# First loads in larger parts by two queues, second group's inputs turned early, all weight sums on GpSimd: a fused attention and feed-forward kernel

## The chip, the cores and the metric

The kernel runs on one core of a Trainium2 chip. The metric is the device time of one execution in microseconds (us). Five engines run their own instruction lists in order and meet only at semaphores: TensorE (PE; its weight loads are shown apart as PEld), VectorE (DVE), ScalarE (ACT), GpSimd (POOL) and SyncE (SP), which here issues nearly all transfers. Transfers are carried by 16 DMA engines that all issuing queues share.

## The reference

Sixteen sequences of 128 rows and 1024 columns pass a cross-attention block and a feed-forward block, each with a residual. All is float32.

```
x = x + Attention(layernorm(x), ctx, ctx)        # Wq, Wk, Wv, Wo with biases
x = x + scale * (x_ei(layernorm(x)) @ kernel)    # kernel is 0/1; inputs beyond 80% of x count -4 times

Attention: Q = query @ Wq + bq      (32 heads of 32)
           K, V = ctx @ Wk + bk, ctx @ Wv + bv   (8 heads, each for 4 query heads)
           softmax(Q K^T / sqrt(32)) V, then @ Wo + bo
```

## The kernel before

**Groups.** Two sequences make a group (`GB = 2`), so there are eight groups. For each group the kernel forms V and K from the context (`prep_v` L404, `prep_k` L393), Q from the normalized rows (`prep_q_plain` L419 for the first group, `prep_q` L485 after it), then softmax and the weighted sum for four pairs of sequence and half of the heads (`attend` L755), then the output projection (`out_proj` L623) and the feed-forward product (`ffn` L738). PE is kept busy by weaving: the projection and feed-forward products of one group are cut in pieces and laid between the softmax steps of another.

**What sets the order.** All instructions after the first loads are put out by hand. A `Stream` (L23) keeps a queue of generators and a list of events with due times. Each piece of PE work adds its estimated microseconds to `now`; an event is put out when `now` passes its due time. The due times thus decide only the place of an instruction in its engine's list. On the chip an engine goes through that list in order and waits wherever its semaphores are not there yet.

**Quadrants.** VectorE transposes blocks of 32 by 32. So that whole tiles can be turned this way, the context and the weights Wk and Wv are loaded by quadrants of 32 partitions: four transfers each (`load_ctx` L147, `load_by_quadrants` L155), every row in runs of 1 KB. `turn_ctx` (L344) turns half a sequence's context in one instruction; a pair of tiles `cT` holds a group's. Rows of x are normalized by `norm_x` (L387): two halves of statistics (L283), their sum (L287), an addition (L289), then `rs_a`, a power on GpSimd (L291), and the scaling on VectorE (L292). VectorE waits for GpSimd between L289 and L292. The first two groups turn x on PE (`turned` L330); later groups send it through DRAM and turn it on VectorE (`rows_x` L356, `through_dram` L302, `turn_x` L366).

**First loads (L185 to L201).** SP, ACT and GpSimd issue in turn: context of sequence 0, Wv in three cuts of its columns of chunks (`2, 4`), context of sequence 1, Wk in two cuts, then the rows of sequences 0 and 1 and the output bias by SP. The identity matrix is made on GpSimd after its share of the loads. Then SP loads eight pieces of Wq (512 KB each, `fetch` L220), four blocks of Wo (`load_o_part` L810), and the context of sequences 2 and 3.

**Weight sums.** Products of Q (from the second group on) and of the output projection use seven instead of eight block products (`seven` L462), with sums of weight blocks. `combine` (L776) forms four sums of a half of Wq or Wo, two instructions of 128x512 each, and stores them in DRAM by SP. Wo's first half (`sums_of_wo` L856), Wq's second half and Wo's second half are formed on GpSimd, Wq's first half on VectorE (`sums_of_wq` L895, L904). They run beside the first group's attention, as do the transposes of the second group's context (due times in L923, L926, L927) and the norms of its rows (L928).

**Third group.** During the second group's attention the rows of the third are loaded, normalized at due times of 10 and 14 us (`get_x` L875), sent through DRAM and turned at 30 to 36 us (`turn_rows` L882); its context is turned at 3.7 to 18 us (L939).

Of the kernel before, what the change touches and what calls it, by code (L numbers as in the profile page):

```python
# [17 lines left out]
P = 128  # L18
# [58 lines left out]
def once(fn, *args):  # L77
    fn(*args)
    yield 0.0
# [3 lines left out]
def kernel(  # L83
# [40 lines left out]
    ps_tp = ctx.enter_context(tc.tile_pool(name="ps_tp", bufs=2, space=PSUM))  # L124
    ps_sc = ctx.enter_context(tc.tile_pool(name="ps_sc", bufs=4, space=PSUM))

# [17 lines left out]
    def load_ctx(b, queues=(nc.sync,)):  # L147
        c_t = work.tile([P, NB, NC, 32], FP, tag="ctx", name=f"ctx{b}", bufs=2)
        src = key_value[b].rearrange("(t r) (k c f) -> k r t (c f)", r=32, k=NB, c=NC)
        for k in range(NB):  # L150
            dst = c_t[k * 32 : (k + 1) * 32].rearrange("r t c f -> r t (c f)")
            queues[k % len(queues)].dma_start(out=dst, in_=src[k])
        cs[b] = c_t

    def load_by_quadrants(dst, w, queues, *cuts):  # L155

        src = w.rearrange("(k c f) n -> k f c n", k=NB, f=32)
        n = 0
        for lo, hi in zip((0,) + cuts, cuts + (NC,)):
            for k in range(NB):  # L160
                queues[n % len(queues)].dma_start(
                    out=dst[k * 32 : (k + 1) * 32, lo:hi], in_=src[k][:, lo:hi]
                )
                n += 1

    def load_x(b, tag="row"):

        x_t = work.tile([P, D], FP, tag=tag, name=f"xn{b}", bufs=2)
        nc.sync.dma_start(out=x_t, in_=x[b])
        xns[b] = x_t  # L170
# [10 lines left out]
            )  # L181

    three = (nc.sync, nc.scalar, nc.gpsimd)  # L185
    load_ctx(0, three)
    load_by_quadrants(wv_sb, Wv, (nc.scalar, nc.gpsimd, nc.sync), 2, 4)
    load_ctx(1, three)
    load_by_quadrants(wk_sb, Wk, (nc.scalar, nc.gpsimd, nc.sync), 4)
    load_x(0)  # L190
    load_x(1)
    ident = const.tile([P, P], FP, name="ident")
    make_identity(nc, ident)
    minus_half = const.tile([P, 1], FP, name="minus_half")
    nc.gpsimd.memset(minus_half, -0.5)

    nc.gpsimd.dma_start(out=bkT, in_=bk)
    nc.gpsimd.dma_start(out=bv_b, in_=bv.partition_broadcast(P))
    nc.gpsimd.dma_start(out=bqT, in_=bq.rearrange("p (a g) -> p a g", a=NA))
# [573 lines left out]
            stream.later(0.7 + 2.4 * i, first)  # L773
        return pts

    def combine(w, k, part, engine=nc.gpsimd):  # L776

        if w == "q":

            a11, a12, a21, a22 = [part[r, o] for o in range(2) for r in range(2)]  # L780
            ops = [(a22, a21, a22, ADD), (a21, a11, a21, SUB), (a11, a22, a11, SUB), (a12, a12, a11, SUB)]
            order = (a22, a11, a21, a12)
        else:
            b11, b12, b21, b22 = [part[r, o] for r in range(2) for o in range(2)]
            ops = [(b11, b12, b11, SUB), (b12, b22, b12, SUB), (b22, b22, b11, SUB), (b21, b21, b22, SUB)]
            order = (b11, b22, b12, b21)
        for dst, left, right, op in ops:
            for h in range(2):
                cols = slice(h * HALF, (h + 1) * HALF)
                engine.tensor_tensor(dst[:, cols], left[:, cols], right[:, cols], op)  # L790
            yield
        for n, t in enumerate(order):
            nc.sync.dma_start(out=sums[w, n + 1, k], in_=t)
# [30 lines left out]
    with tc.manual_schedule():  # L824
# [8 lines left out]
        for grp in range(NGRP):  # L833
            os[grp] = out_proj(grp)
            if grp + 2 < NGRP:
                qs[grp + 2] = prep_q(grp + 2)
        for _ in range(RING):
            fetch()
        o_parts = [load_o_part(0)]

        def plain(a):
            return prep_q_plain(a, {(r, k): at_q[r, a, k] for r in range(2) for k in range(2)})
# [3 lines left out]
                turn_ctx(j, h)  # L846
            stream.add(prep_v(0, [j]))
        stream.add(prep_k(0))
        for j in range(GB):
            load_ctx(GB + j)  # L850
        stream.run(0.0, lambda: len(stream.queue) > 1)
        nc.vector.tensor_scalar_mul(bqs, bqT, scale)
        for j in range(GB):
            norm_x(j)

        def sums_of_wo():  # L856
            def inputs():
                for j in range(GB):
                    load_x(GB + j, "turn")
                load_ffn()  # L860

            def then():
                o_parts.append(load_o_part(1))

            stream.later(10.0, inputs)
            stream.later(8.0, lambda: spread(combine("o", 0, o_parts[0]), 3.3, then))

        stream.add(prep_x(0, 0), prep_x(0, 1), once(sums_of_wo), plain(0))
        stream.run(0.0, lambda: stream.queue)

        def norms(grp, *us):
# [3 lines left out]
        def get_x(grp):  # L875

            for j in range(GB if grp < NGRP else 0):
                b = grp * GB + j
                load_x(b, "turn")
                stream.later((10.0 if grp == 2 else 5.0) + 4.0 * j, lambda b=b: rows_x(b))  # L880

        def turn_rows(grp):  # L882
            for n, at in enumerate((30.0, 32.0, 34.0, 36.0)):
                stream.later(at, lambda n=n: turn_x(grp * GB + n // 2, n % 2))

        def get_ctx(grp):
# [8 lines left out]
        def sums_of_wq(k):  # L895
            def then():
                for _ in range(4):
                    fetch()
                if k == 1:
                    spread(combine("o", 1, o_parts[1]), 3.3)  # L900

            part = {(r, o): pieces[at_q[r, o, k]] for r, o in BLOCKS}
            if k == 0:
                spread(combine("q", k, part, nc.vector), 1.5, then)  # L904
            else:
                spread(combine("q", k, part), 3.3, then)

        def between(gen, n, fn, *args):

# [5 lines left out]
        for grp in range(NGRP):  # L915
            b0, b1, nxt = grp * GB, grp * GB + 1, grp + 1
            p0, p1 = b0 - 2, b0 - 1
            first, more = grp == 0, nxt < NGRP
            last = grp == NGRP - 1
            length = 17.4 if first else 23.2 if grp < NGRP - 2 else 21.0  # L920
            if first:
                stream.add(
                    once(prep_ctx, nxt, 12.5, 13.5),  # L923
                    between(plain(1), 9, sums_of_wq, 0),
                    once(sums_of_wq, 1),
                    once(turn_ctx, nxt * GB, 1),  # L926
                    once(turn_ctx, nxt * GB + 1, 1),  # L927
                    once(norms, nxt, 5.0, 10.0),  # L928
                    prep_k(nxt),
                    once(get_ctx, nxt + 1),  # L930
                    prep_v(nxt),
                    prep_x(nxt, 0),
                    prep_x(nxt, 1),
                    once(convert_ffn),
                    between(qs[nxt], 40, residuals, grp),
                )
            elif more:
                stream.add(
                    *([once(get_x, nxt), once(prep_ctx, nxt, 3.7, 8.0, 13.0, 18.0)] if grp == 1 else []),  # L939
                    once(turn_rows, nxt),  # L940
                    os[grp - 1],
                    once(get_ctx, nxt + 1),
                    prep_k(nxt),
                    once(load_residual, b0, 4.0),
                    prep_v(nxt),
                    qs[nxt],
                    once(get_x, nxt + 1),
                    once(prep_ctx, nxt + 1, 2.5, 7.0, 11.0, 16.0),
                    ffn(p0),
                    once(load_residual, b1, 2.0),  # L950
                )
                if nxt < NGRP - 1:
                    stream.add(ffn(p1))
            else:
                stream.add(
                    os[grp - 1],
                    mixed(ffn(p1 - 2), ffn_transpose(p0), 10, 2),
                    once(load_residual, b0, 2.0),
                    mixed(ffn(p0), ffn_transpose(p1), 8, 2),
                    once(load_residual, b1, 2.0),  # L960
                )
            if not more:
                for q in range(2 * NA):
                    b, a = grp * GB + q % GB, q // GB
                    start = stream.now
                    pts = attend(b, a, 15.0)
                    stream.later(15.0, lambda b=b, a=a, pts=pts: weighted(b, a, pts) or 1.0)
                    stream.run(start + 12.0)
                stream.drain()
                break  # L970
            for q in range(2 * NA):
                b, a = grp * GB + q % GB, q // GB
                start = stream.now
                pts = attend(b, a, length)
                if q == 2 * NA - 1:
                    stream.run(start + length - 2.0, lambda: stream.queue)
                else:
                    stream.run(start + length - 2.0)
                stream.run(stream.now, lambda: None in pts)
                weighted(b, a, pts)  # L980
                stream.now += 1.0
# [56 lines left out]
```

## Time and profile before

| | |
|---|---|
| median of 3 runs | 792.11 us (790.93 to 792.24) |
| the profiled execution's own time | 790.87 us |
| its span, first to last instruction | 789.1 us |
| PE busy | 767.6 us (97%) |
| DVE, ACT, POOL busy | 485.6, 322.7, 113.3 us |
| DMA, mean over the span | 241 GB/s |
| granted PE clock | full in every slice |

The profile page gives the busy time of each engine, the span in 40 slices, the chain of work that ended last, and groups of instructions by line. Its rows can be listed in order of time (the timeline): start, length, engine, line, operation, what is written and read, how many, and in brackets how long the engine sat idle before and what released it. A line with `SPq` or `DMA` is an issue or a transfer. All times count from the span's start.

### The profile page before, as it was taken

The page shows a single profiled execution, that of the slowest core. Times are in us where ns is not written, and L with a number is a line of the kernel's source. Part 1 is how long each engine was busy: PE and PEld are TensorE (multiplying, and loading weights), DVE is VectorE, ACT ScalarE, POOL GpSimd, SP SyncE. Part 2 cuts the span into 40 slices and gives each one's busy share as a digit, 9 for nine tenths or more (in the row PEclk, how much of TensorE's full clock was granted, in tenths as well). Part 3 has the DMA queues.
Part 4 walks back from the last instruction along what each step waited for, and adds up shares of the span by engine and source line. Part 5 has one row for each costly group of instructions (what it writes and reads, how often), then busy time and mean ns, then how long its engine had stood idle before and what let it go on. Part 6 is the DMA issues. An engine that isn't in the chain of part 4 may idle for free.

```text
span 789.1 us, 13748 instructions
## 1 busy us (share of the span) xinstructions
PE 767.6 (97%) x5024; PEld 572.0 (72%) x5024; DVE 485.6 (62%) x882; ACT 322.7 (41%) x1261; POOL 113.3 (14%) x142
## 2 busy tenths in 40 slices
PE   5998999999999999999999999999999999999997
PEld 4886884589746996479855898568974799546566
DVE  1258748756766667466684667755676756667442
ACT  0254754434344343344433444343434445466100
POOL 4143703020010102020020200102001200100300
PEclk9999999999999999999999999999999999999999
DMA  9999799987698776888788796977769567562512
GB/s 236 350 314 309 277 338 388 283 225 266 224 316 217 248 238 229 298 213 260 221 256 274 197 285 218 306 222 214 257 226 315 194 203 249 178 200 81 198 42 81
DMA packets 97828, 190.32 MB, mean 241 GB/s; under 512 B 8080, under 2 KB 56272, under 8 KB 97760
## 3 DMA queue, kind: packets, MB, share of 16 engines
q1 hardware_dynamic: 96128, 187.33, 74.2%
q0 software_dynamic: 528, 1.12, 0.6%
q10 hardware_dynamic: 1104, 0.98, 0.6%
q8 instruction: 40, 0.66, 0.3%
q14 instruction: 28, 0.23, 0.1%
HBM read 160.04 MB, written 29.36 MB: 240 GB/s over the span
## 4 chain that ended last, share of the span: by engine, by line
PE 84%; DMA 7%; DVE 3%; SPq 2%; POOL 1%; issue 1%; ACT 1%; POOLq 0%
PE f L323 15%; PE o_u L662 13%; PE q_u L451 12%; PE o_v L662 7%; PE tpp L601 6%; PE q_v L451 6%; PE v L323 5%; PE k L323 5%; PE sc L568 4%; PE av L611 4%; PE o_c L662 3%; PE q_c L451 3%; DMA wo<-in_L_xattn_Wo_dram 2%; SPq L225 1%; DMA piece<-in_L_xattn_Wq_dram 1%
## 5 line engine op out<-in xcount | busy, mean ns | idle before, releaser
L584 ACT ACTIVATE p<-sc,negm 128x128 f32<-128x128 f32 x512 | 181.5, 369 | 140.3 <-DVE negm L580 76.8
L603 ACT COPY pt<-tpp 128x512 f32<-128x512 f32 x128 | 74.5, 591 | 142.9 <-PE tpp L601 142.6
L580 DVE TENSOR_REDUCE negm<-sc 128x4 f32<-128x512 f32 x128 | 86.6, 679 | 53.7 <-PE sc L568 53.6
L584 ACT ACTIVATION_READ_ACCUMULATOR p<-sc,negm 128x1 f32 x512 | 105.4, 206 | 0.0
L323 PE MATMUL f<-wf_sb,x2l 128*128 128x512 f32 x256 | 104.8, 409 | 0.0
L323 PE MATMUL f<-wf_sb,x2h 128*128 128x512 f32 x256 | 100.5, 393 | 0.0
L596 DVE TENSOR_TENSOR p<-p,inv 128x512 f32<-128x512 f32 x128 | 91.9, 718 | 4.4
L451 PE MATMUL q_u<-t,piece 128*128 128x128 f32 x672 | 80.9, 275 | 0.0
L601 PEld LDWEIGHTS tpp<-ident,p 128*128 128x128 f32 x512 | 61.9, 141 | 25.6 <-issue 17.0
L601 PE MATMUL tpp<-ident,p 128*128 128x128 f32 x512 | 75.9, 273 | 4.5 <-DVE p L596 3.1
L451 PEld LDWEIGHTS q_u<-t,piece 128*128 128x128 f32 x672 | 77.9, 192 | 0.0
L180 POOL TENSOR_TENSOR x<-x,bo_b 128x256 f32<-128x256 f32 x64 | 55.1, 887 | 151.3 <-DMA x<-in_x_dram 99.4
L323 PE MATMUL v<-wv_sb,cT 128*128 128x256 f32 x256 | 61.4, 388 | 9.5 <-DMA wv_sb<-in_L_xattn_Wv_dram 7.4
L662 PE MATMUL o_v<-piece,s 128*128 128x512 f32 x128 | 60.4, 598 | 0.5 <-DVE x L676 0.5
L662 PE MATMUL o_u<-piece,s 128*128 128x512 f32 x128 | 59.1, 594 | 0.7 <-DVE x L676 0.7
L323 PEld LDWEIGHTS v<-wv_sb,cT 128*128 128x128 f32 x256 | 47.8, 194 | 16.3 <-DVE cT L349 9.4
L323 PE MATMUL k<-cT,wk_sb 128*128 128x256 f32 x256 | 58.1, 380 | 1.3 <-DVE cT L349 1.3
L662 PE MATMUL o_u<-piece,yT 128*128 128x512 f32 x128 | 58.5, 599 | 0.0
L323 PEld LDWEIGHTS f<-wf_sb,x2l 128*128 128x128 f32 x256 | 48.2, 188 | 10.4 <-issue 1.1
L323 PEld LDWEIGHTS k<-cT,wk_sb 128*128 128x128 f32 x256 | 47.9, 190 | 10.5 <-issue 2.6
L323 PEld LDWEIGHTS f<-wf_sb,x2h 128*128 128x128 f32 x256 | 48.2, 188 | 9.4 <-issue 0.5
L568 PEld LDWEIGHTS sc<-kT,qT 32*128 32x128 f32 x1024 | 31.4, 186 | 25.7 <-issue 25.7
(86 smaller groups left out, 936.3 us busy)
## 6 DMA issues: line engine op xcount, KB each, us to landing
piece<-o SPq DMA_DIRECT2D x64, 512.0 KB, 4.8
piece<-q SPq DMA_DIRECT2D x56, 512.0 KB, 5.1
piece<-in_L_xattn_Wq_dram SPq DMA_DIRECT2D x50, 512.0 KB, 5.3
piece<-in_L_xattn_Wo_dram SPq DMA_DIRECT2D x48, 512.0 KB, 4.6
xn<-in_x_dram SPq DMA_DIRECT2D x16, 512.0 KB, 6.8
x<-in_x_dram SPq DMA_DIRECT2D x16, 512.0 KB, 4.8
ctx<-in_ctx_dram SPq DMA_DIRECT2D x60, 128.0 KB, 7.0
out_dram<-x SPq DMA_DIRECT2D x15, 512.0 KB, 2.7
```

The lines of the kernel that those rows point to most:

```text
L180: lambda cut=cut: nc.gpsimd.tensor_add(x_t[:, cut], x_t[:, cut], bo_b[:, cut]) and None,
L225: nc.sync.dma_start(out=t.rearrange("p (c n) -> p c n", c=src.shape[1]), in_=src)
L323: nc.tensor.matmul(mm, lhsT=lhsT, rhs=rhs, start=k == 0, stop=k == n - 1)
L451: nc.tensor.matmul(mm if part is None else mm[:, part], lhsT=lhsT, rhs=rhs, start=start and n == k == 0, stop=k == len(some) - 1, skip_gro ...
L568: nc.tensor.matmul(tiles[i][:, g], lhsT=qT[rows, g], rhs=kT[rows, a, cols], start=True, stop=True,)
L580: nc.vector.tensor_reduce(negm, tile_, AX.X, ALU.max, negate=True)
L584: nc.scalar.activation(p[:, g], tile_[:, g], AF.Exp, bias=negm[:, g : g + 1], accum_out=total[:, g : g + 1],)
L596: nc.vector.tensor_mul(p, p, inv.unsqueeze(2).to_broadcast([P, NG, S]))
L601: nc.tensor.transpose(tp[:, g], p[:, g], ident)
L603: nc.scalar.copy(pt, tp)
L611: nc.tensor.matmul(mm[i * HD : (i + 1) * HD], lhsT=vs[b][:, h * HD : (h + 1) * HD], rhs=pts[i], start=True, stop=True,)
L662: nc.tensor.matmul(mm, lhsT=lhsT[:, 2 * k + c], rhs=w[:, c], start=start and k == c == 0, stop=k == c == 1, skip_group_check=True,)
```

## The change

Six edits, all of which act on what is put out before the third group's attention:

1. The first loads are issued by SP and ACT alone. Wv and Wk go in four parts of 256 KB each, without cuts. The rows of sequence 0 are issued before Wk, those of sequence 1 after it. The identity is made first of all on GpSimd.
2. The context of sequences 2 and 3 is loaded after six of the eight Wq pieces, before the last two and before Wo; the rows of sequences 2 and 3 directly after Wo.
3. The four transposes of the second group's context are put out while the first group's Q is formed (`prep_ctx, 1` beside `plain(0)`).
4. All sums of `combine` are formed on GpSimd, Wq's first half too.
5. The norms of the second group's rows come at other due times (12 and 24 us after the first attention step begins; before, 5 and 10 us after the second half of the first group's Q).
6. For the third group, rows are normalized 8 us later, context is turned at 5 to 24 us instead of 3.7 to 18, rows are turned 5 us later.

```diff
-    def load_by_quadrants(dst, w, queues, *cuts):
+    def load_by_quadrants(dst, w, queues):
...
-    three = (nc.sync, nc.scalar, nc.gpsimd)
-    load_ctx(0, three)
-    load_by_quadrants(wv_sb, Wv, (nc.scalar, nc.gpsimd, nc.sync), 2, 4)
-    load_ctx(1, three)
-    load_by_quadrants(wk_sb, Wk, (nc.scalar, nc.gpsimd, nc.sync), 4)
+    two = (nc.sync, nc.scalar)
+    load_ctx(0, two)
+    load_by_quadrants(wv_sb, Wv, two)
+    load_ctx(1, two)
     load_x(0)
+    load_by_quadrants(wk_sb, Wk, two)
     load_x(1)
...
-        for _ in range(RING):
+        for _ in range(RING - 2):
+            fetch()
+        for j in range(GB):
+            load_ctx(GB + j)
+        for _ in range(2):
             fetch()
         o_parts = [load_o_part(0)]
+        for j in range(GB):
+            load_x(GB + j, "turn")
...
-            stream.later(8.0, lambda: spread(combine("o", 0, o_parts[0]), 3.3, then))
+            stream.later(9.0, lambda: spread(combine("o", 0, o_parts[0]), 3.3, then))
-        stream.add(prep_x(0, 0), prep_x(0, 1), once(sums_of_wo), plain(0))
+        stream.add(prep_x(0, 0), prep_x(0, 1), once(sums_of_wo),
+            once(prep_ctx, 1, 5.0, 7.0, 9.0, 11.0), plain(0))
...
-                stream.later((10.0 if grp == 2 else 5.0) + 4.0 * j, lambda b=b: rows_x(b))
+                stream.later((18.0 if grp == 2 else 5.0) + 4.0 * j, lambda b=b: rows_x(b))
...
             for n, at in enumerate((30.0, 32.0, 34.0, 36.0)):
+                at += 5.0 if grp == 2 else 0.0
...
-            if k == 0:
-                spread(combine("q", k, part, nc.vector), 1.5, then)
-            else:
-                spread(combine("q", k, part), 3.3, then)
+            spread(combine("q", k, part), 2.7, then)
...
-                    once(prep_ctx, nxt, 12.5, 13.5),
+                    once(norms, nxt, 12.0, 24.0),
                     between(plain(1), 9, sums_of_wq, 0),
                     once(sums_of_wq, 1),
-                    once(turn_ctx, nxt * GB, 1),
-                    once(turn_ctx, nxt * GB + 1, 1),
-                    once(norms, nxt, 5.0, 10.0),
                     prep_k(nxt),
...
-    *([once(get_x, nxt), once(prep_ctx, nxt, 3.7, 8.0, 13.0, 18.0)] if grp == 1 else []),
+    *([once(get_x, nxt), once(prep_ctx, nxt, 5.0, 9.0, 14.0, 24.0)] if grp == 1 else []),
```

More of the change, by code (lines that the diff above doesn't have):

```diff
@@ L125 @@
     ps_sc = ctx.enter_context(tc.tile_pool(name="ps_sc", bufs=4, space=PSUM))
+    ident = const.tile([P, P], FP, name="ident")
+    make_identity(nc, ident)
+    minus_half = const.tile([P, 1], FP, name="minus_half")
+    nc.gpsimd.memset(minus_half, -0.5)
     wk_sb = const.tile([P, NC, KV], FP, name="wk_sb")
@@ L153, in load_ctx @@
         cs[b] = c_t
-    def load_by_quadrants(dst, w, queues, *cuts):
+    def load_by_quadrants(dst, w, queues):
         src = w.rearrange("(k c f) n -> k f c n", k=NB, f=32)
[L158 to L164, printed above, removed]
+        for k in range(NB):
+            queues[k % len(queues)].dma_start(out=dst[k * 32 : (k + 1) * 32], in_=src[k])
     def load_x(b, tag="row"):
@@ L181, in load_residual @@
             )
-    three = (nc.sync, nc.scalar, nc.gpsimd)
-    load_ctx(0, three)
-    load_by_quadrants(wv_sb, Wv, (nc.scalar, nc.gpsimd, nc.sync), 2, 4)
-    load_ctx(1, three)
-    load_by_quadrants(wk_sb, Wk, (nc.scalar, nc.gpsimd, nc.sync), 4)
+    two = (nc.sync, nc.scalar)
+    load_ctx(0, two)
+    load_by_quadrants(wv_sb, Wv, two)
+    load_ctx(1, two)
     load_x(0)
+    load_by_quadrants(wk_sb, Wk, two)
     load_x(1)
[L192 to L195, printed above, removed]
     nc.gpsimd.dma_start(out=bkT, in_=bk)
@@ L774, in attend, with combine @@
         return pts
-    def combine(w, k, part, engine=nc.gpsimd):
+    def combine(w, k, part):
         if w == "q":
@@ L789, in combine @@
                 cols = slice(h * HALF, (h + 1) * HALF)
-                engine.tensor_tensor(dst[:, cols], left[:, cols], right[:, cols], op)
+                nc.gpsimd.tensor_tensor(dst[:, cols], left[:, cols], right[:, cols], op)
             yield
@@ L848 @@
         stream.add(prep_k(0))
-        for j in range(GB):
-            load_ctx(GB + j)
         stream.run(0.0, lambda: len(stream.queue) > 1)
-        nc.vector.tensor_scalar_mul(bqs, bqT, scale)
         for j in range(GB):
             norm_x(j)
+        nc.vector.tensor_scalar_mul(bqs, bqT, scale)
         def sums_of_wo():
[L857 to L860, printed above, removed]
             def then():
                 o_parts.append(load_o_part(1))
-            stream.later(10.0, inputs)
-            stream.later(8.0, lambda: spread(combine("o", 0, o_parts[0]), 3.3, then))
-        stream.add(prep_x(0, 0), prep_x(0, 1), once(sums_of_wo), plain(0))
+            stream.later(10.0, load_ffn)
+            stream.later(9.0, lambda: spread(combine("o", 0, o_parts[0]), 3.3, then))
+        stream.add(
+            prep_x(0, 0),
+            prep_x(0, 1),
+            once(sums_of_wo),
+            once(prep_ctx, 1, 5.0, 7.0, 9.0, 11.0),
+            plain(0),
+        )
         stream.run(0.0, lambda: stream.queue)
```

## The prediction

> **What bounds the kernel now.** I read PE's waits first, then PE's timeline, then the stretches of the start.
>
> PE's waits over the whole span (total, times, longest; two more rows are of 0.5 and 0.3 us):
>
> ```profile
> PE v L323 <- DMA wv_sb<-in_L_xattn_Wv_dram: 7.4, 2, 7.0
> PE tpp L601 <- DVE p L596: 3.1, 2, 2.6
> PE v L323 <- DVE cT L349: 2.1, 1, 2.1
> PE tpp L601 <- DVE x2l L717: 1.4, 1, 1.4
> PE k L323 <- DVE cT L349: 1.3, 1, 1.3
> PE o_u L662 <- DVE x L676: 0.7, 1, 0.7
> PE o_v L662 <- DVE x L676: 0.5, 1, 0.5
> ```
>
> PE is the bound (767.6 of 789.1 us busy). Only these waits can be won, and the change reaches all but the 1.4 us, which lie at the end. PE's own list has the same instructions in the same order after the change, so its work costs the same. The waits' places, in PE's timeline:
>
> ```profile
> 6.99 3.61 PE L323 MATMUL v<-wv_sb,cT 128*128 128x256 f32 x8 [6.99 <-DMA wv_sb<-in_L_xattn_Wv_dram]
> ...
> 15.10 3.72 PE L323 MATMUL v<-wv_sb,cT 128*128 128x256 f32 x16 [2.07 <-DVE cT L349]
> 18.65 7.07 PE L323 MATMUL k<-cT,wk_sb 128*128 128x256 f32 x32
> ...
> 64.05 5.45 PE L323 MATMUL k<-cT,wk_sb 128*128 128x256 f32 x24 [1.29 <-DVE cT L349]
> ...
> 80.15 0.63 PE L601 MATMUL tpp<-ident,p 128*128 128x128 f32 x4 [2.65 <-DVE p L596]
> ```
>
> K of the first group begins at 18.65 with no wait; from there PE never idles 0.3 us until 64. So the whole start counts by one number: when K begins. After that: 1.29 and 0.45 + 2.65 us at 62 to 80, and 1.24 us at 136 to 142.
>
> **The start (edit 1).** Stretches: length, busy times, then granted clock, DMA share, GB/s:
>
> ```profile
> 2.00:10.00 8.00, 3.01 (x7) 2.50 (x8) 1.31 (x2) 0.00 (x0) 7.05 (x16) 1.00 1.05 246
> 10.00:16.00 6.00, 3.47 (x14) 2.28 (x14) 1.64 (x3) 1.28 (x1) 0.00 (x0) 1.00 1.11 216
> 38.00:42.00 4.00, 4.00 (x26) 3.28 (x28) 0.00 (x0) 0.79 (x3) 1.96 (x3) 1.00 1.08 199
> 21.00:31.00 10.00, 9.76 (x53) 8.47 (x53) 3.19 (x6) 3.06 (x6) 1.12 (x2) 1.00 1.10 348
> ```
>
> The DMA engines are full in all four, yet the rate differs: 246 GB/s with quadrant loads from three queues, 216 mostly from two, 199 from SP alone (context), 348 for Wq pieces on all 128 partitions in the same 1 KB runs. So the destination of 32 partitions sets the rate. [...] I take 208, between the one- and the two-queue row; bounds 199 and 239 (the mean from 2 to 17 us before).
>
> Data flows from 2.0 us. Wv has landed after 0.52 (context) + 1.05 + 0.13 MB (the bias, beside them): 2.0 + 1.70/0.208 + 0.25 (landing) = 10.4. V takes as long as K, whose 32 matmuls run from 18.65 to 25.56: 6.9 and, since the second context lands at 12.9 and is turned by 13.7, runs through: PE is ready for K at 17.4. Wk comes after the second context and the rows of sequence 0: 3.28 MB by quadrants, 0.52 MB of rows at 0.4 (the 406 GB/s of the rows before): 2.0 + 15.75 + 1.3 + 0.25 = 19.3. K begins at 19.3 instead of 18.65: **+0.65**. With 239 it is 17.3 (-1.35), with 199 it is 20.0 (+1.35). What is late next is Wk, because rows went in front of it: that alone costs 1.3. [...] The norms of both rows (statistics to scaling 3.3 us each, from 17.6 on) end near 24, before K does at 26.2: hidden; x1 lands by 20.6.
>
> **Order of pieces, early transposes (edits 2, 3).** Six Wq pieces, then 1 MB of context at 199 (5.3 us), lands near 36.5. Four transposes at 0.69 = 2.8 us fall into VectorE's empty stretch from 25.7 to 42.9 (17.3 us before the first maximum): free. The K wait of **1.29** goes. Wq's last two pieces come at 39, needed at 50; Wo's last part at 44.5 to 45.5 instead of 41.7, which delays GpSimd, not PE; the rows of sequences 2 and 3 behind it by 48 (1.3 us each), asked for at 56.6.
>
> **Sums on GpSimd (edits 4, 5).** The rows: VectorE's eight sum instructions cost 6.2 us there (mean 817 ns). GpSimd's timeline:
>
> ```profile
> 41.80 7.39 POOL L790 TENSOR_TENSOR wo<-wo,wo 128x512 f32<-128x512 f32 x6 [2.04 <-DMA wo<-in_L_xattn_Wo_dram]
> 57.52 2.65 POOL L790 TENSOR_TENSOR piece<-piece,piece 128x512 f32<-128x512 f32 x2 [8.33 <-PE q L323]
> ...
> 76.51 5.85 POOL L790 TENSOR_TENSOR piece<-piece,piece 128x512 f32<-128x512 f32 x4
> ```
>
> 1.23 us per instruction beside a quiet VectorE, 1.46 beside a busy one (single ones 1.27 or 1.72). [...]
>
> The danger is order. Each `rs_a` stands in GpSimd's list, and VectorE stands still until it is done. New list on GpSimd: 8 for Wo, 2 for Wq, `rs_a` of sequence 2, 10 for Wq, `rs_a` of sequence 3, 4 for Wq. On VectorE the norm of sequence 2 now stands after the fourth product with 1/sum (56.6 before), that of sequence 3 after the second one of the next step.
> - Wo's sums: 45.5 + 6 x 1.23 = 52.9, two more to 55.5. VectorE asks for the first `rs_a` at 58.3, so nobody waits: a cover of 2.8 us. Then GpSimd goes on at 58.9 with ten sums: 12.3 us and three meetings of 0.45 = 13.6, to 72.5.
> - VectorE meanwhile: scaling to 60.7, maxima from 61.0 (63.93 before), exponentials on ScalarE from 61.7, two products done by 67.3, statistics to 69.0. Then it stands until `rs_a` is done at 73.1, about 4 us. Behind it: scaling (to 74.8), fourth maximum (75.4), third product (76.7 with a meeting). Also ScalarE's fourth exponential stands behind that maximum.
> - PE: K from 60.77 for 6.9, then transposes and V between; it reaches the third transpose at 73.0 and waits to 76.7 (3.7 us). Fourth at 78.9, no more wait; the weighted sum at 80.3, where it was 81.57. So 1.29 + 0.45 + 2.65 of waits go, 3.7 come with small gaps between: **-1.25**. Bounds: ten sums at 1.23 give -2.6, at 1.6 (nearest the 1.72) +1.0.
>
> The weight sums themselves are ready earlier than before (last Wq sum 78.5 instead of 82.3), also Wo's second half (90 instead of 94.3). Meetings after 90 fall away: the 0.32 wait at 101 may go, **-0.2**. SP's queue: the stores of Wq's first sums hold it from 59 to 67.5; behind them stand four Wq pieces, needed at 84 and landing at 76, then context needed at 125.
>
> **Third group (edit 6).** PE at 136.7 waited 0.71 and at 141.8 waited 0.53, both for an addition that stood behind a norm (3.0 us from statistics to scaling) on VectorE. In the new list both additions stand ahead of the norms: **-1.2** (bounds -1.24 and 0). The price: rows of sequence 5 come back from DRAM behind eight context loads on SP, near 164; VectorE may stand 2 us from 162 for them, ahead of what PE needs at 168 (the next sums of rows at 176). Counted at nothing, up to 1 if they come at 167. Not seen in the trace.
>
> **Sum.** +0.65 - 1.25 - 0.2 - 1.2 = **-2.0 us**. The profiled span would go from 789.1 to 787.1, its own time from 790.87 to 788.9. The median of the runs is 792.11, so 790.1.
>
> **Rivals.**
> - *Two queues carry as much as three* (239 GB/s): K begins at 17.3, 2.0 better than forecast: 788.1. For it: 246 GB/s began as 237 in its first 2 us, when GpSimd's queue had hardly come in. Against it: 216 and 199.
> - *The gain becomes a new wait*: GpSimd's ten sums take 15 us instead of 13.6 (1.5 each, as in Wo's second half now), and the start runs at 199: 790.1 + 1.4 + 0.7 = 792.2, no difference that can be told. For it: the standing VectorE is the longest new wait and passes to PE one for one. Against it: while VectorE stands it meets nobody.
> - *Slower: the first loads.* [...] Each part of K's delay passes to PE. At 160 GB/s Wk lands at 2.0 + 20.5 + 1.55 = 24.0, +4.75 over the forecast: 794.9. It decides from 169 GB/s down (K at 22.9, total +1.6). For it: in the SP-only stretch single microseconds went to 173, and at 10 to 16 the rate fell as Wv and Wk came in. Against it: no stretch of 4 us lies under 199.
>
> **How the numbers follow.** A measurement of this kernel can tell 0.2% (1.6 us) from no change. Forecast 0.48 (of it 0.32 beyond 0.2%, 0.16 within), two queues as good as three 0.2 (faster), gain becomes a wait 0.12 (within), slow loads 0.2 (slower, with a late return of sequence 5 in the same share). So faster 0.52, same 0.28, slower 0.2. Low end: start at 239 (-2.0) and the sums at their best bound (-1.35) give 790.1 - 3.35, near 787.0; 5 in 100 lie below. High end: into the slow-loads case, 794.0, some 14 in 100 above.
>
> **What would show it.** K's first matmul: 19.3, released by Wk, not by context. No wait for cT at 62. VectorE idle some 4 us before the scaling of sequence 3, released by `rs_a`; the third transpose of that step waits about 3.7. No wait at L662 near 136 to 142. I am wrong if K starts past 22 or before 18, if VectorE stands at the first `rs_a` already (Wo later than 48), or if PE waits anew after 150.

## The result

The changed kernel takes 796.42 us (median of 4 runs, 795.53 to 797.32), the kernel before it, on the same chip, 791.56 us (790.93 to 792.24). The ratio is 1.0062, its 95% interval 1.0048 to 1.0076: slower by some 4.9 us, where 2.0 us faster was forecast. The profiled execution took 797.32 us with a span of 795.6 us.

### The profile page after: what moved, and what is told of

It reads as the page before. It is cut to its first block, busy times and chain, and to the rows that moved or that the text cites. A ratio compares the mean times of both kernels' runs of the same rounds, so it can differ in the third digit from the quotient of the medians.

```text
span 795.6 us, 13726 instructions
## 1 busy us (share of the span) xinstructions
PE 770.2 (97%) x5024; PEld 574.1 (72%) x5024; DVE 479.1 (60%) x874; ACT 322.4 (41%) x1261; POOL 119.1 (15%) x141
## 4 chain that ended last, share of the span: by engine, by line
PE 88%; DMA 5%; DVE 3%; POOL 2%; ACT 2%; issue 1%; ACTq 0%; SPq 0%; POOLq 0%
PE f L316 15%; PE o_u L655 14%; PE q_u L444 11%; PE o_v L655 7%; PE tpp L594 6%; PE q_v L444 6%; PE v L316 6%; PE k L316 5%; PE sc L561 4%; PE av L604 4%; PE o_c L655 3%; PE q L316 3%; PE q_c L444 2%; POOL piece L783 2%; DMA wv_sb<-in_L_xattn_Wv_dram 1%; DMA turn_x<-dram_x 1%
## 5 line engine op out<-in xcount | busy, mean ns | idle before, releaser
L316 PE MATMUL f<-wf_sb,x2l 128*128 128x512 f32 x256 | 105.4, 412 | 0.0
L316 PE MATMUL f<-wf_sb,x2h 128*128 128x512 f32 x256 | 101.1, 395 | 0.0
L594 PEld LDWEIGHTS tpp<-ident,p 128*128 128x128 f32 x512 | 62.5, 142 | 25.6 <-issue 17.1
L594 PE MATMUL tpp<-ident,p 128*128 128x128 f32 x512 | 76.3, 274 | 4.7 <-DVE p L589 3.3
L316 PE MATMUL v<-wv_sb,cT 128*128 128x256 f32 x256 | 62.4, 395 | 13.0 <-DMA wv_sb<-in_L_xattn_Wv_dram 13.0
L316 PEld LDWEIGHTS v<-wv_sb,cT 128*128 128x128 f32 x256 | 49.1, 199 | 19.3 <-issue 13.0
L316 PE MATMUL k<-cT,wk_sb 128*128 128x256 f32 x256 | 57.9, 380 | 0.8 <-DVE v L405 0.8
L316 PEld LDWEIGHTS f<-wf_sb,x2l 128*128 128x128 f32 x256 | 48.2, 188 | 11.0 <-issue 1.1
L316 PEld LDWEIGHTS f<-wf_sb,x2h 128*128 128x128 f32 x256 | 48.2, 188 | 10.2 <-issue 0.5
L316 PEld LDWEIGHTS k<-cT,wk_sb 128*128 128x128 f32 x256 | 47.9, 190 | 10.0 <-issue 2.6
```

Of the source, the lines that this page charges most:

```text
L316: nc.tensor.matmul(mm, lhsT=lhsT, rhs=rhs, start=k == 0, stop=k == n - 1)
L594: nc.tensor.transpose(tp[:, g], p[:, g], ident)
```

## The profile after

Line numbers are seven lower than before (L323 is now L316, L601 is L594). PE's waits over the whole span of the changed kernel:

```profile
PE v L316 <- DMA wv_sb<-in_L_xattn_Wv_dram: 13.0, 1, 13.0
PE tpp L594 <- DVE p L589: 3.3, 1, 3.3
PE q_c L444 <- DVE v L405: 1.8, 1, 1.8
PE tpp L594 <- DVE x2l L710: 1.4, 1, 1.4
PE k L316 <- DVE v L405: 0.8, 1, 0.8
PE av L604 <- ACT pt L596: 0.6, 1, 0.6
```

The forecast waits are gone: the K wait on `cT`, both waits at the additions, and 0.45 of the two transposes. One long wait of 3.3 us stands in for the 2.65, as forecast (3.7). Two rows are new: 13.0 us at the start for Wv, and 1.8 us before Q of the third group. The same places in PE's timeline (start, length, then what, and in brackets the wait ahead of it):

```profile
13.01 9.04 PE L316 MATMUL v<-wv_sb,cT 128*128 128x256 f32 x32 [13.01 <-DMA wv_sb<-in_L_xattn_Wv_dram]
22.86 7.14 PE L316 MATMUL k<-cT,wk_sb 128*128 128x256 f32 x32 [0.81 <-DVE v L405]
...
64.98 7.17 PE L316 MATMUL k<-cT,wk_sb 128*128 128x256 f32 x32
...
75.45 1.89 PE L316 MATMUL v<-wv_sb,cT 128*128 128x256 f32 x8
...
80.65 0.63 PE L594 MATMUL tpp<-ident,p 128*128 128x128 f32 x4 [3.30 <-DVE p L589]
81.11 3.03 PE L316 MATMUL v<-wv_sb,cT 128*128 128x256 f32 x8
...
177.29 2.94 PE L444 MATMUL q_c<-xT,piece 128*128 128x128 f32 x24 [1.78 <-DVE v L405]
```

Two things are to be seen besides the waits. K begins at 22.86, not at 19.3. And the same eight V matmuls take 1.89 us at 75.45 and 3.03 us at 81.11, just behind the long wait. Likewise V of the first group takes 9.04 us where 6.9 was reckoned: its first eight matmuls are 0.427 us apart, later ones 0.216. (The wait ahead of K names `v`, but that addition was over at 22.51; the last part of Wk landed at 22.77.)

PE's list is the same in both kernels, so each matmul can be set against its twin. How much later each place is reached, in the two profiled executions:

| place | shift after it | step's own part | forecast |
|---|---|---|---|
| K of the first group begins | +4.21 | +4.21 | +0.65 |
| second attention step done (85 us) | +4.35 | +0.14, of it half clock some +1.7 | -1.25 |
| weighted sum at 105 | +4.61 | +0.26 | -0.2 |
| additions at 140 and 145 | +2.84 | -1.77 | -1.2 |
| Q of the third group | +5.24 | +2.4 | 0, up to +1 |
| last matmul | +6.74 | +1.5, in the feed-forward products | 0 |

(Half clock is a stretch in which PE is granted half its clock; here 0.50 from 81.71 to 85.12. From the third transpose to the end of the step PE takes 4.53 us here, from 80.65 to 85.18, and 2.85 in e2, described below, which has no half clock there.)

The last row is not scatter between two executions. From 180 us on only the feed-forward products (`f`) go slower. Their rows on the two pages, first before, then after (busy us, mean ns of one):

```profile
L323 PE MATMUL f<-wf_sb,x2l 128*128 128x512 f32 x256 | 104.8, 409 | 0.0
L323 PE MATMUL f<-wf_sb,x2h 128*128 128x512 f32 x256 | 100.5, 393 | 0.0
...
L316 PE MATMUL f<-wf_sb,x2l 128*128 128x512 f32 x256 | 105.4, 412 | 0.0
L316 PE MATMUL f<-wf_sb,x2h 128*128 128x512 f32 x256 | 101.1, 395 | 0.0
```

From one start to the next it is 229.7 ns before and 233.4 after, the mean of 426 neighbouring pairs; the other products keep their pace (K 215.9 ns, V 216.8). The experiments below tell with which edit this goes.

The profile before was below all four timed runs of its kernel, and this one is the highest of its four: the profiles differ by 6.45 us, the medians by 4.9.

## Experiments

Each set shared one chip and the runs of the kernel before: 791.44 us (40 runs) for the first four kernels, 791.87 us (51 runs) for the next four, 791.98 us (20 runs) for the last four.

### The loads alone, and everything but the loads

`e1_loads_alone`: the kernel before with edit 1 only.

> The kernel before with edit 1 alone (two queues, 256 KB parts, rows ahead of Wk). Theory: the start is where the time went, because the last DMA ring to finish a part lags the mean by some 3 us and PE then starts with its clock at half: K of the first group starts at 22.9 as in the changed kernel, and the later waits stay as before (1.3 and 2.7 us near 64 and 80), so the time is that of before + 4.2 (795.8). Rival (the later edits are to blame, the start is absorbed by slack behind it): within 1.5 us of before.

Measured: 795.71 us (794.02 to 797.46), ratio 1.0062 (1.0046 to 1.0077). `e2_loads_undone`: the changed kernel with the first loads of before.

> The changed kernel with the first loads of before. Theory: V starts at 7.0, K at 18.7, so 4.2 us go: near 792.2, within 1 us of the kernel before, since the other edits lose as much as they win. Rival (the gains forecast for the other edits are there): 788 to 789.

Measured: 790.92 us (788.04 to 793.14), ratio 0.9994 (0.9983 to 1.0005). So edit 1 by itself costs what the whole change costs, and the other five edits together are worth 0.5 us by the medians, which this cannot tell from nothing. In e1's trace K begins at 20.72 and not at 22.9, so the start costs 2.1 us there; 0.45 of it is won back by 145 us, and 1.5 come after 180 us. The expected total was met with a part of it in another place. In e2's trace the shift against before is -0.97 us after the second attention step and -3.15 after the additions; Q of the third group gives 2.0 of it back (a wait of 1.4 and smaller ones), and after 180 us nothing is lost. The loads and the third group were thus separate losses.

**The slower feed-forward products come with edit 1.** From start to start they take 233.3 to 233.4 ns in the changed kernel, e1, e3 to e8 and e11, and 229.7 in before, e2, e10 and e12; that is 1.5 us in all. Of what edit 1 changes, e5 has three queues again, e6 the small parts and e7 the rows behind Wk, and all three are slow. What the slow kernels share, and the others lack, is the identity made ahead of the loads. In the code `ident` and `minus_half` (one column) are then also taken from the pool `const` ahead of `wf_sb`, the operand of these products. That the place of `wf_sb` in memory is the reason is not shown; no run moves the one without the other.

### What in the loads

The changed kernel with one property of its loads taken back at a time. `e5_three_queues`:

```diff
-    two = (nc.sync, nc.scalar)
-    load_ctx(0, two)
-    load_by_quadrants(wv_sb, Wv, two)
-    load_ctx(1, two)
+    three = (nc.sync, nc.scalar, nc.gpsimd)
+    turn = (nc.scalar, nc.gpsimd, nc.sync)
+    load_ctx(0, three)
+    load_by_quadrants(wv_sb, Wv, turn)
+    load_ctx(1, three)
     load_x(0)
-    load_by_quadrants(wk_sb, Wk, two)
+    load_by_quadrants(wk_sb, Wk, turn)
```

> The changed kernel, with its first context and weight loads dealt to three queues again (GpSimd's the third), the 256 KB parts and the rows ahead of Wk as changed. Three accounts of the start's loss of some 4 us (V at 12 to 13 instead of 7, K at 20.8 to 22.9 instead of 18.65). (a) The number of queues: with three some 240 GB/s instead of 213, so the last part of Wv lands near 10.5, V begins there, K near 20: some 794.0. (b) The size of the parts: each part ends on its slowest ring and V waits for all eight columns, so the third queue changes little: V still at 12, 796. (c) The rows ahead of Wk: V earlier, K unchanged at 22 or later: 796. I expect (a) and (b) half each: V near 11, K near 20.5, 794.5.

Measured: 794.15 us (790.57 to 798.54), ratio 1.0026 (1.0013 to 1.0039). `e6_small_parts`, two queues, cuts as before (`load_by_quadrants` takes them again):

```diff
-    load_by_quadrants(wv_sb, Wv, two)
+    load_by_quadrants(wv_sb, Wv, two, 2, 4)
...
-    load_by_quadrants(wk_sb, Wk, two)
+    load_by_quadrants(wk_sb, Wk, two, 4)
```

> The changed kernel on its two queues, with Wv cut in three and Wk in two parts per quadrant as before the change; rows still ahead of Wk. If the size of the parts is what delays V (account b), its first columns are there near 8 and V begins then, cold, with its cold stretch inside the wait for the later columns, as in the kernel before; V would end near 19.5 and K be bound by Wk, near 20.5 to 21: 794.3. If the number of queues is it (account a), Wv's last columns land at 12 to 13 as now and V ends near 17.5 to 18 (warm by then), but Wk still lands at 21 to 22.8 and K starts with it: 795.8. I expect V's start near 8 and K near 21: 794.8.

Measured: 793.23 us (791.22 to 794.74), ratio 1.0014 (1.0004 to 1.0025). `e7_wk_first` puts `load_x(0)` behind Wk.

> The changed kernel with the rows of sequence 0 behind Wk instead of ahead of it, so Wk has 0.26 MB less in front: it lands some 1.2 us earlier. V starts as now (12 to 13) and, cold, takes 9, so the TensorE is free for K at 21 to 22: the account that charges the rows (1.3 us in the prediction) expects K 1.3 earlier and 795.0; the account by which V's late and cold start sets K as much as Wk does expects 0 to 0.8 earlier: 795.9. I expect the second.

Measured: 793.98 us (791.02 to 797.00), ratio 1.0027 (1.0016 to 1.0038). `e8_warm_start` puts 70 transposes of the identity at the head of PE's list.

> The changed kernel with 70 transposes of the identity at the head of TensorE's list, into a tile that nobody reads, so that the engine works while it waits for Wv. If the cold clock is what makes V take 9 us instead of 6.9, V takes 6.9 to 7 here and is done 1.9 earlier; K then starts with Wk, at 20.7 to 22: gain 0.5 to 1.9, 795.2. If V's 9 us come from something else (operands that arrive late), V stays at 9 and the time at 796.4. I expect the first.

Measured: 795.12 us (793.00 to 795.61), ratio 1.0041 (1.0029 to 1.0053). The starts, from the traces:

| kernel | last part of Wv | V begins | V ends | last part of Wk | K begins |
|---|---|---|---|---|---|
| before | 10.92 | 6.99 | 18.8 | 17.25 | 18.65 |
| changed | 12.76 | 13.01 | 22.05 | 22.77 | 22.86 |
| loads alone (e1) | 11.78 | 12.03 | 20.9 | 20.19 | 20.72 |
| three queues (e5) | 11.60 | 11.69 | 21.8 | 20.65 | 21.59 |
| small parts (e6) | 11.14 | 7.03 | 18.1 | 19.81 | 17.96 |
| Wk first (e7) | 11.43 | 11.68 | 21.8 | 18.96 | 21.65 |
| warm start (e8) | 11.90 | 12.28 | 19.35 | 20.12 | 20.22 |

V and K in e6 and in e8 (PE's timeline):

```profile
7.03 4.08 PE L322 MATMUL v<-wv_sb,cT 128*128 128x256 f32 x8 [7.03 <-DVE cT L348]
11.38 1.97 PE L322 MATMUL v<-wv_sb,cT 128*128 128x256 f32 x8 [0.27 <-DMA wv_sb<-in_L_xattn_Wv_dram]
14.41 3.72 PE L322 MATMUL v<-wv_sb,cT 128*128 128x256 f32 x16 [1.06 <-DVE cT L348]
17.96 7.39 PE L322 MATMUL k<-cT,wk_sb 128*128 128x256 f32 x32
```

```profile
12.28 7.07 PE L316 MATMUL v<-wv_sb,cT 128*128 128x256 f32 x32
20.22 7.15 PE L316 MATMUL k<-cT,wk_sb 128*128 128x256 f32 x32 [0.87 <-DMA wk_sb<-in_L_xattn_Wk_dram]
```

The table settles the start, as far as one trace of each kernel can.

- *Size of the parts:* it is what delays V. In e6, two queues bring all of Wv by 11.14, hardly later than three did before, and V begins at 7.03, with the first chunks. Each uncut part holds all chunks of one quadrant, and in the program each V matmul reads a chunk over all four quadrants. In the four rows with uncut parts and no warm start V began 0.09 to 0.25 us after the last part had landed. That I expected V near 8 and K near 21 was near for V and too late for K: Wk is cut as well, its first four parts had landed by 17.57, and K began at 17.96, ahead of the last part (19.81).
- *Number of queues:* three queues with uncut parts leave V at 11.69. That account falls, as does the forecast of K near 20.5.
- *Rows ahead of Wk:* in e7 Wk lands at 18.96, and K still begins at 21.65, when V is done. The rows cost nothing while V is this late. (In the changed kernel's own trace Wk, at 22.77, ended 0.7 us behind V.)
- *Cold clock:* with PE at work before V, V takes 7.07 us, as reckoned. In the other kernels with uncut parts it takes 8.9 to 10.1; in the changed one the first eight matmuls, 0.427 us apart instead of 0.216, lie ahead of the first full-clock record at 16.86. K then waits for Wk, so little of it is gained in the end, as the timed runs say.

The timed gains are smaller than the starts, and e5 to e8 all keep the 1.5 us in the feed-forward products. e6 begins K 4.9 us ahead of the changed kernel's profile, and its ratio is only 0.0048 lower, 3.8 us (a different chip and set). Its trace shows a half-clock stretch at 75.8 and waits of 3.2, 0.7 and 0.5 us behind it. e5 and e7, whose K is not early, also came out lower than the changed kernel's four runs; by how much their start differs from it on average, the profiles of one execution each don't say.

### The third group's rows

`e3_rows_back_first`: the changed kernel with the fourth group's context issued behind the return of the third group's rows.

```diff
                     os[grp - 1],
-                    once(get_ctx, nxt + 1),
+                    *([once(get_ctx, nxt + 1)] if grp != 1 else []),
                     prep_k(nxt),
                     once(load_residual, b0, 4.0),
                     prep_v(nxt),
+                    *([once(get_ctx, nxt + 1)] if grp == 1 else []),
```

> The changed kernel, with the context loads of the fourth group issued behind the return of the third group's rows from DRAM instead of ahead of it. Theory: VectorE's 6.3 us wait for the rows of sequence 5 falls below 2 us, PE's wait at the third group's q_c (1.8 us, plus 0.4 behind it) goes, so 2.0 to 2.2 us less than the changed kernel: 794.3. Rival (the rows are late by DRAM or by the late norm, not by SP's order): the wait stays over 4 us and the time at 796.4.

Measured: 793.50 us (789.96 to 795.00), ratio 1.0019 (1.0008 to 1.0030). SP's queue in the changed kernel, then VectorE there:

```profile
157.32 8.44 SPq L157 DMA_DIRECT2D ctx<-in_ctx_dram  x8
165.80 2.02 SPq L304 DMA_DIRECT2D turn_x<-dram_x  x4
```

```profile
162.86 0.71 DVE L364 STREAM_TRANSPOSE xT<-turn_x 128x512 f32<-128x512 f32 x1 [2.49 <-DMA turn_x<-dram_x]
...
172.53 0.71 DVE L364 STREAM_TRANSPOSE xT<-turn_x 128x512 f32<-128x512 f32 x1 [6.27 <-DMA turn_x<-dram_x]
...
176.86 0.38 DVE L405 TENSOR_TENSOR v<-v,bv_b 128x256 f32<-128x256 f32 x1
```

The issues of eight context loads hold SP's queue for 8.44 us, and the rows of sequence 5 are asked for only at 165.8. VectorE stands 6.27 us for them, and behind it in its list stands the addition at L405 that frees the accumulator for which PE waits at 177.29. The same in e3:

```profile
155.45 1.73 SPq L304 DMA_DIRECT2D turn_x<-dram_x  x4
...
166.01 4.22 SPq L157 DMA_DIRECT2D ctx<-in_ctx_dram  x8
```

The rows are asked for 10 us earlier, VectorE no longer stands for sequence 5, and PE's waits list no `q_c`. In this trace the start is 2.1 us late instead of 4.2, so only the stage is compared: from the additions to Q of the third group the shift stays at -1.56, where the changed kernel lost 2.4.

### The wait before the third transpose, and the clock behind it

`e4_wait_filled`: 24 transposes of the identity in that wait, into a tile that is overwritten.

> The changed kernel with 24 transposes of the identity (2.6 us of PE work whose result is overwritten) put into PE's list where it waits 3.3 us for the third product of the second attention step. Theory: the wait of over 3 us sets PE's clock to half for 3.4 us and costs 1.5 us on top of itself; filled, the V matmuls behind it run at 379 ns again and the time falls by 1.5 us to 794.9, though work was added. Rival (the long matmuls there have another cause, such as the weights' reads): the same long matmuls and up to 0.5 us more, 796.4 to 796.9.

Measured: 793.08 us (790.98 to 795.98), ratio 1.0025 (1.0013 to 1.0038). The rest of the wait is 0.77 us and the eight matmuls behind it take 1.89. Its time is lower than expected by 1.8; V's start was 1.3 us earlier than in the changed kernel's profile, and the wait for `v` at the third group only 0.3.

The cause of the wait is on GpSimd (its timeline in the changed kernel), with VectorE behind it:

```profile
62.88 13.67 POOL L783 TENSOR_TENSOR piece<-piece,piece 128x512 f32<-128x512 f32 x10
76.50 0.55 POOL L284 TENSOR_TENSOR rs_a<-ve_a,minus_half 128x1 f32<-128x1 f32 x1
```

```profile
77.09 1.74 DVE L285 TENSOR_SCALAR xn<-xn,mv_a,rs_a 128x1024 f32<-128x1024 f32 x1 [3.73 <-POOL rs_a L284]
```

This is what was forecast: ten additions in 13.6 us, VectorE standing some 4 us. What comes behind it was not. Stretches of the changed kernel, granted clock in the third column from the end:

```profile
76.00:80.00 4.00, 1.35 (x7) 0.84 (x5) 2.87 (x4) 0.47 (x3) 4.00 (x5) 1.00 1.06 346
80.00:84.00 4.00, 3.35 (x13) 2.71 (x14) 1.93 (x4) 1.99 (x8) 3.92 (x5) 0.71 1.09 213
84.00:88.00 4.00, 4.00 (x49) 2.65 (x47) 0.42 (x1) 1.17 (x2) 4.00 (x4) 0.86 0.97 358
```

The clock records put half clock from 81.71 to 85.12. It costs some 1.7 us, more than the forecast gain of this stage.

### The changes without the losses

`e9_before_loads` is e3 with the first loads of before.

> The changed kernel with two of its edits taken back: the first loads as before the change, and the fourth group's context behind the return of the third group's rows. Account of the parts: start +0, middle -1.3 (a wait of 3.5 before a transpose of the second attention step stays, and in most executions one window of 3.4 us at half clock follows it, +1.5), additions -1.7, third group 0. Against the kernel before: -1.5 to -3, so 789.5; more than 1.0 better than the changed kernel with before's loads alone. A rival, that the third group's transposes become late in another place once the context goes behind the rows, expects no better than that kernel, 791.

Measured: 789.73 us, ratio 0.9971 (0.9962 to 0.9981), as the account of the parts expected. Fourteen runs lie at 787.43 to 792.28; the profiled one took 1999.99 us and is not read, so e9 has no trace. `e10_norm_early` is e9 with one due time changed:

```diff
-                    once(norms, nxt, 12.0, 24.0),
+                    once(norms, nxt, 12.0, 16.0),
```

> The kernel e9 with the normalisation of sequence 3 due 8 us earlier (16 instead of 24), which puts its one small GpSimd operation behind two instead of eight of the additions that form Wq's sums. If the row that says that VectorE stood 3.7 us for that operation is the cause of the 3.3 to 3.5 us wait before the third transpose, the wait falls below 1 us and no window at half clock follows: 2.5 us less than e9, and 1 more in most executions: 786.5. If the wait is the softmax's own (scores, exponentials), it stays and the time is e9's; a normalisation that now comes ahead of the softmax can cost up to 1 us at the first transpose (787.5).

Measured: 787.81 us (785.64 to 789.81), ratio 0.9947 (0.9929 to 0.9966). The wait is where it was placed, in GpSimd's order: VectorE now stands 0.67 us, PE 1.12 us at the first transpose and not at the third. But the gain was 1.9 us by the medians and not 2.5 to 3.5. The six runs fall into two groups: 785.6 to 786.2 with a mean granted clock of 1.000, which is what was expected, and 789.5 to 789.8 with 0.995 to 0.998. The profiled one is the highest. PE's waits and timeline there:

```profile
PE q_u L451 <- DMA piece<-q: 1.9, 1, 1.9
...
PE tpp L601 <- DVE p L596: 1.1, 1, 1.1
```

```profile
93.56 0.70 PE L451 MATMUL q_u<-t,piece 128*128 128x128 f32 x4 [1.91 <-DMA piece<-q]
```

PE now comes earlier to the products that need Wq's sums, and these are not back from DRAM: GpSimd finishes them at 81.6, and SP stores the last ones at 82.65, behind eight context issues of 8.84 us. A half-clock stretch from 94.09 to 97.50 follows this wait; another lies from 15.59 to 19.00. `e11_small_parts_norm_early` is e10 with e6's loads.

> The kernel e10 with its first loads on two queues in parts cut as before the change (rows ahead of Wk), as in e6. K began 0.7 to 1.1 us earlier in e6's profile than with three queues. If the two queues cost nothing once the parts are small, this is e10's time less 0.5 to 1: 785.9. If something else in e6 ran slower than its start shows (its timed runs were 2 us above the kernel with three queues), it is 1 to 2 above e10: 788.

Measured: 787.83 us (786.95 to 788.94), ratio 0.9950 (0.9938 to 0.9961). The time is that of e10, neither the 0.5 to 1 us better nor the 1 to 2 worse. The account that something else in e6 ran slower was right in kind: e11 too makes the identity ahead of its loads, its feed-forward products take 233.3 ns, and its trace, 3.39 us ahead of before at 180 us, ends 1.89 ahead. So this pair doesn't compare the queues alone. `e12_wq_on_vector` is e9 with edit 4 taken back (the first half of Wq's sums on VectorE, the due times of both halves as before).

> The kernel e9 with edit 4 alone taken back: the first half of Wq's sums on VectorE again (four double additions), the second half on GpSimd. The account in which GpSimd's ten queued additions make the 3.5 us wait expects that wait to fall, but VectorE then has the additions in front of its softmax, which the kernel before shows as waits of 0.4 and 2.65: in all within 1 us of e9, 789. The account by which the move to GpSimd is what gains in the middle expects 1 to 1.5 more than e9: 790.8.

Measured: 787.22 us (786.43 to 790.18), ratio 0.9950 (0.9935 to 0.9964). Both accounts missed it: it is 2.5 us below e9 (the intervals just touch). Its PE waits:

```profile
PE tpp L601 <- DVE p L596: 2.1, 1, 2.1
...
PE tpp L601 <- ACT p L584: 0.6, 1, 0.6
```

The waits of this stage are 2.7 us, against 3.5 in e2; there is no wait for Wq's sums, and no half clock behind them. From K's start to the end of the stage e12 wins 2.05 us on before, e2 1.40. Edit 4 thus cost time. That `rs_a` stands behind ten additions accounts for it, as e10, which keeps edit 4 and moves `rs_a`, comes out as low; e9 has no trace to set beside them. e10, e11 and e12 beat both kernels by some 0.5%; which of the three is best, these runs don't tell.

## Why the prediction was wrong, point by point

**Start, the first failing step.** "Wv has landed ... 10.4", "V takes as long as K ... 6.9", "PE is ready for K at 17.4", K bound by Wk at 19.3. The rate was about right: 208 GB/s assumed, and the changed kernel's stretches (GB/s last) show

```profile
2.00:10.00 8.00, 0.00 (x0) 0.00 (x0) 1.30 (x2) 0.00 (x0) 1.90 (x5) 1.00 1.01 213
10.00:16.00 6.00, 2.99 (x7) 2.49 (x8) 0.40 (x1) 1.28 (x1) 0.00 (x0) 1.00 1.11 217
16.00:20.00 4.00, 4.00 (x18) 3.43 (x18) 1.33 (x3) 0.00 (x0) 0.00 (x0) 1.00 1.13 211
```

Two terms were not. A mean rate did not say when a part is whole: in these traces a part lands in 16 shares, and not together. In the changed kernel's trace the first share of Wv's last parts is there 2.9 to 4.0 us ahead of the last one (0.6 to 2.5 in the other kernels with uncut parts); in e6's small parts at most 1.2. By 12.76 some 2.30 MB had been moved (10.76 us at 214 GB/s), where 1.70 MB had to be there: the rest went into transfers queued behind (the first shares of the second context landed from 11.12 on). So landing was 12.76 there and 11.4 to 11.9 in the other kernels with uncut parts, +1.0 to +2.4. Wk, forecast for 19.3, landed at 22.77 in the same way, and at 19.9 to 20.4 in the traces of e1, e3, e4 and e8, which issue the same loads; in e1, e3 and e4 the end of V decides. And V's 6.9 us was taken from K, which before ran wholly at full clock (matmuls 0.216 us apart). Before the change V's cold first matmuls lay between its waits for Wv and the second context (three waits, 9.5 us with the first), and cost nothing; now V begins when all is there, and all its cold time (1.8 to 3.1 us over e8's 7.07) is on the path. e8 takes just that away. In the traces with uncut parts and no warm start K is late by 2.1 to 4.2 us, not by 0.65. I had costed the loss of the cuts at nothing, although the row with V at 6.99 showed that PE worked while Wv was still landing: the cover that was removed.

The rival "the first loads" was right in its place and wrong in its cause; it asked for a rate below 169 GB/s, and the changed kernel's rows above show 211 to 217. It would give 794.9: near the result, by luck. With quadrants alone or nearly so (2 to 10 us) three queues carried 246 GB/s before and 226 in e5, two queues 211 in e1, 213 in the changed kernel and 225 in e6.

**PE's own work, the second failing step.** "PE's own list has the same instructions in the same order after the change, so its work costs the same." The list is the same, the cost is not: the feed-forward products take 3.6 ns more each, 1.5 us in all, with the identity made first. The prediction put this at nothing.

**K wait and early transposes:** right; the 1.29 us went, in e2, e3 and the changed kernel alike.

**Sums on GpSimd:** the mechanism and its sizes held (13.67 us for ten, 3.73 us standing, 3.3 to 3.5 us at the third transpose in the changed kernel, e2 and e3; without the clock the stage gives some -1.5 in the profile pair, -1.40 in e2, -1.52 in e3). No run shows singly the three meetings of 0.45 us that the forecast adds; the ten sums took 1.37 us each. The step that missed is that the 3.3 us wait had a tail: half clock behind it, some +1.7 (e3's wait of 3.4 had none). And e12, with -2.05, shows that edit 4 took from this gain; the other edits made it.

**Weighted sum, -0.2:** +0.26 in the changed kernel's profile and +0.26 to +0.36 in e5 to e7; about -0.4 in e2, e3, e4, e8 and e12. Half clock lies ahead of it in the first four, but in e8 as well, so the clock alone doesn't explain the loss. PE's wait is for ScalarE's copy `pt` in both kernels, not for a meeting of GpSimd and VectorE; why ScalarE is late in four traces stays open.

**Additions, -1.2:** right, -1.77 (-0.97 and -0.80; the waits' small surroundings went with them).

**Return of sequence 5, "counted at nothing, up to 1 if they come at 167":** they came by 172.5 and cost 2.4. The mechanism was named; the eight context issues were sized too short (8.44 us in SP's queue), and e3 removes it.

That e2, the change without its loads, lies at 790.92, near 790.1, is luck: without the start -2.65 us was forecast, and e2 is 0.5 below its kernel before, since half clock (a mean clock below 0.999 in 12 of its 14 runs) and the third group took the rest. Edit 1 put 4 to 5 us on top, at the start and in the feed-forward products.

## What to carry to other kernels

Count a load by what its consumer can begin with: here cutting the transfers let V begin at 6.99 and 7.03 instead of 11.7 to 13.0, and so hid both the rest of the landing and PE's cold clock; the 213 and 225 GB/s of the changed kernel and e6 did not show that. When an edit takes a wait apart or moves it, ask what was hiding inside the wait. A small operation (here `rs_a`, 0.55 us) was as late as everything queued ahead of it on GpSimd (ten additions, 13.67 us), and one due time (e10) or one half of the work on the other engine (e12) was worth some 2 us, as much as the edits that e9 keeps. And the same list of instructions did not cost the same: with a tile made at another place in the program the products from 180 us on came 233.4 ns apart instead of 229.7, which the comparison from start to start showed.

## What the runs showed of the hardware

**In these traces half clock lies on a grid of 3.413 us.** The lengths of all full-clock stretches between the first record and the last half-clock one, and of all half-clock stretches in the middle, are multiples of 3.413 us (64.85 = 19 x 3.4133 and 709.97 = 208 x 3.4133 in the changed kernel, 778.24 = 228 x 3.4133 before). I laid this grid over 13 traces and added up PE's idle time in each window, from the first one at full clock on. Windows with 1.90 and 2.04 (e10), 2.35 (the changed kernel), 2.88 (e7), 3.04, 3.07 and 3.41 us of idle time (e5, e6, e8) were followed by a window at half clock; those with up to 1.86 us never. So in e10 a wait of 1.91 us at 91.65 was enough, a window 56% idle, and in e2 one of 3.5 us, cut into 1.86 and 1.66, was not.

Much of the scatter within one kernel goes with it. The mean granted clock was at least 0.999 in 38 of 111 runs of the kernel before, with a median of 790.76 us, and lower in the other 73, with 792.13. In the kernels whose trace has a wait of 2.9 to 3.9 us in the second attention step (the changed one, e2, e3, e5 to e8) 19 of 103 runs have a clock that high; in those where it is short (e4, e11, e12), 20 of 22. That each lower clock is such a stretch was seen only in the profiled executions.

**V's slow first stretch ends on this grid too.** It lasted until the end of the first window that PE filled (idle for at most 0.31 us; windows with 0.77 us and more didn't end it): 3.5 to 3.9 us in e1, e3 and the changed kernel (V takes 8.9 to 9.0), some 6 us in e4, e5 and e7 (10.1).

Open is why the feed-forward products take 233.4 ns instead of 229.7 when the identity is made first, and why the timed gain of e6 is smaller than its earlier start.
